# Three attention heads of four turned on VectorE and by SBUF to SBUF transfers, in a fused Perceiver, Mamba and MoE layer

## The chip, the cores and the metric

The kernel runs on one core of a Trainium2 chip. The metric is the device time of one execution in microseconds; the median of the runs shown is quoted. A core has TensorE (PE in the profile, its weight loads PEld), VectorE (DVE), ScalarE (ACT), GpSimd (POOL) and SyncE (SP), each of which works through its own instructions in order, and 16 DMA engines. Nearly all transfers of this kernel are issued by SyncE, one after the other.

## What is computed

All numbers are float32. Only the first of three stages is touched by the change, cross-attention of 16 sequences of 128 queries over 2048 context rows, 16 heads of 32:

```python
x = x + xattn(layernorm(x), ctx)          # x (16,128,512), ctx (16,2048,512)
x = x + mamba_block(layernorm(x))         # in_proj, conv, scan over 16 states, out_proj, MLP
x = x + moe(layernorm(x))                 # 8 experts' gates, one shared and one expert weight

# xattn
q = queries @ wq.T + bq
k = context @ wk.T + bk
v = context @ wv.T + bv
attn = softmax(q k^T * HD ** -0.5)        # per head
out = (attn v) @ wo.T + bo
```

## The kernel before

The order of the work is written out by hand: a loop over time steps u (line 1329) issues on every engine what belongs to that step, and each engine takes its instructions in the order in which they were issued. Steps 0 to 255 are the attention: step u is sequence u // 16, block u // 4 % 4 of 512 context rows, and head group u % 4, four heads. Beside it runs the rest: keys and values of the next block (group "made"), from step 54 on the scan of the Mamba stage for pairs of sequences ("decays", "inputs", "scan"), and "late" work put at fixed steps (queries, output projection, in-projection, out-projection). After step 256 come the remaining scans and the feed-forward.

**One attention step.** `scores` (L302): four matmuls, one for each head, into four PSUM banks of 512 columns. `weighted` (L378): the weighted sums of step u-1 for the heads turned on TensorE, and of step u-2 for the heads turned by transfer. `maxima` (L312): VectorE takes the row maximum of each bank (L315). `exps` (L319): ScalarE takes the exponential of each bank into `pr` (L325). The exponentials must be turned, with context rows on partitions, before they can be weights of the sums. Two ways are used for it, with ND = 2 and NP = 4 - ND = 2:
- `turn` (L353): heads 0 to NP-1, four 128x128 transposes a head on TensorE (L357) and a copy by ScalarE into `pT` (L359).
- `blocks` (L334): the last ND heads, one VectorE instruction that transposes 32x32 blocks into `tr` (L337, one buffer), which goes to a DRAM tile `trd` (L341, one transfer). `gathered` (L343), in the next step: four transfers bring it back, blocks in their places, as `pd` (L347).

**Keys and values.** A block's 512x512 context product is done in seven products of quarter size (a Strassen-like scheme) instead of eight, for keys in steps with u % 4 = 1 and 2, for values in those with 3 and 0. `load_ctx` (L151) loads the four quarters c00, c10, c11, c01 of the block's context, 256 KB each; c01 has one buffer, the others two. `ctx_sums` (L225) forms four differences on GpSimd in steps u % 4 = 1 (L236): t1 = c01 - c00, t2 = c11 - t1, t3 = c11 - c01, t4 = c10 - t2; in steps with u % 16 = 5 all four stand together, otherwise `dt_third` and `inputs` of the scan (L686 to L698) stand between t2 and t3. `product` (L238) puts products into two PSUM banks, pa and pc (L244). In a step, `x_products` come after the sums (phase 0: c00 and c10; phase 1: t3 into pa, t1 into pc), `y_products` at the end of the step (phase 0: t2 into pa; phase 1: t4 into pa, c11 into pc). `hold` (L282) copies pa to SBUF on ScalarE (L285), and `k_sum` (L253) and `v_sum` (L268) add pc and a held copy on VectorE (L264, L274), with the key bias bk in L264. `y_sums` (L295) writes the last quarter from pa on ScalarE (L262, L272).

**SyncE's order in a step** is that of the calls: `gathered(u-1)`, `step_loads` (L1338: x, dt weights, the scan's row broadcast `bc` at offset 0, L647, 512 KB), then, after the transpose of the step, `trd`, and `later_loads` (L1343: `bc` at offset 16, weights, context). Context quarters are asked for in these steps:

```python
if u % 4 == 1 and made + 1 < B * SB:
    load_ctx(made + 1, ("c00", "c10", "c11"))
if u % 4 == 2 and made + 1 < B * SB:
    load_ctx(made + 1, ("c01",))
```

with made = (u + 3) // 4, so each quarter is asked for three or four steps before it is used.

**The scan's time step.** `dt_first` (L662) takes |v|, exp(-|v|) on ScalarE and max(v, 0) on VectorE (L672); `dt_second` (L677) takes the logarithm into a tile of its own, `l`. `values_kept` (L362) copies the value columns that the transferred heads of head group 3 need one step longer.

Of the kernel before, what the change touches and what calls it, by code (L numbers as in the profile page):

```python
# [15 lines left out]
P = 128  # L16
# [15 lines left out]
ND = 2  # L32
# [4 lines left out]
def perceiver_layer(ctx: ExitStack, tc: tile.TileContext, a: dict, out: bass.AP):  # L37
# [23 lines left out]

    trd = [dram.tile([P, ND * 512], FP, tag=f"trd{i}", name=f"trd{i}") for i in range(2)]

# [49 lines left out]
    with ExitStack() as es:  # L113
# [15 lines left out]
        banks = [psum.tile([P, 512], FP, tag=f"s{j}", name=f"bank{j}") for j in range(4)]  # L129
# [21 lines left out]
        def load_ctx(g, names=("c00", "c10", "c11", "c01")):  # L151

            for n in names:
                j, c = int(n[1]), int(n[2])
                t = pool.tile(
                    [P, 2, 256], FP, tag=n, name=f"{n}_{g}", bufs=1 if n == "c01" else 2
# [68 lines left out]
        def ctx_sums(g, names):  # L225
            b11, b12, b21, b22 = (ctx_t[g, j, c] for j in range(2) for c in range(2))
            for n in names:
                t = pool.tile([P, 2, 256], FP, tag=n, name=f"{n}_{g}", bufs=1)
# [24 lines left out]
        def k_sum(g, o, c, pc, x):  # L253
            for r in range(2):
                hg = 2 * o + r
                if (g, hg) not in kts:
                    kts[g, hg] = pool.tile(
                        [P, 512], FP, tag=f"kt{hg}", name=f"kt{g}_{hg}", bufs=1 + (hg == 3)
                    )
                t = kts[g, hg][:, c * 256 : (c + 1) * 256]  # L260
                if pc is None:
# [20 lines left out]
        def hold(key, g, pa, tag):  # L282
            n = ND if tag == "tr" else 1
            t = pool.tile([P, 2 * n, 256], FP, tag=tag, name=f"{tag}{key}{g}", bufs=1)[:, 0:2, :]
            nc.scalar.copy(t, pa)  # L285
            held[key] = t
# [8 lines left out]
        def y_sums(of, g, ph, pa, pc, tag="u2"):  # L295
            if ph == 0:
                hold(of + "u2", g, pa, tag)
# [4 lines left out]
        def scores(u):  # L302
# [7 lines left out]
            del kts[u // 4, hg]  # L310

        def maxima(u):  # L312
            b, sb, hg = split(u)
            for j in range(4):
                nc.vector.tensor_reduce(  # L315
                    stats[b][0][j][:, sb, hg : hg + 1], banks[j], AX.X, ALU.max, negate=True
                )

        def exps(u):  # L319
# [3 lines left out]
            for j in range(4):  # L323
# [5 lines left out]
                    bias=nm[j][:, sb, hg : hg + 1],  # L329
# [4 lines left out]
        def blocks(u):  # L334
# [6 lines left out]
            nc.sync.dma_start(trd[u % 2], t.rearrange("p c h i q -> p (c h i q)"))  # L341

        def gathered(u):  # L343

            pd = pool.tile([P, 4, ND, 4, 32], FP, tag="pd", name=f"pd{u}", bufs=1)
            for c in range(4):
                nc.sync.dma_start(  # L347
                    pd[c * 32 : (c + 1) * 32].rearrange("k a h i q -> k a (h i q)"),
                    trd[u % 2].rearrange("(a k) (c r) -> c k a r", k=32, c=4)[c],
                )  # L350
            pds[u] = pd
# [41 lines left out]
        def weighted_out(u):  # L393
            b, sb, hg = split(u)
            if hg == 3:
                t = keep.tile([P, 4, P], FP, tag="avs", name=f"avs{b}_{sb}", bufs=4)
                nc.scalar.copy(t[:, 0:3, :], avp[:, 0:3, :])
                nc.scalar.copy(t[0 : NP * HD, 3, :], avp[0 : NP * HD, 3, :])
                avs[b, sb] = t

        def weighted_last(u):
            b, sb, hg = split(u)
            if hg == 3:
                nc.scalar.copy(avs[b, sb][NP * HD :, 3, :], avp[NP * HD :, 3, :])
# [9 lines left out]
        def normal(b):  # L414
# [10 lines left out]
            nm = [keep.tile([P, SB, 4], FP, tag=f"nm{j}", name=f"nm{b}_{j}") for j in range(4)]  # L425
# [34 lines left out]
        def joined(b):  # L460
# [3 lines left out]
            for j in range(4):  # L464
                nc.vector.tensor_copy(
# [1073 lines left out]
```

## Time and profile before

| what | value |
|---|---|
| median of 3 runs | 3578.6 us (3576.97 to 3579.74) |
| the profiled execution's own time | 3579.3 us |
| its span in the trace | 3577.5 us |
| granted TensorE clock, mean | 0.995 of full speed |
| busy: TensorE, VectorE, GpSimd, ScalarE | 98%, 75%, 69%, 64% |
| DMA: bytes moved, mean rate | 816.79 MB, 228 GB/s |
| one cycle of 32 steps with scans | 367.0 us |
| in a cycle: DMA busy share, rate | 79%, 249 GB/s |

The busy share of an engine is an average over the stages. A group of instructions is named by its line, engine and operation, and by the tiles that it writes and reads. The chain of waits follows the work that ended last back in time, at each step to what released it. A timeline row gives start, length, engine, line, operation, tiles, count, and in brackets the idle time before it with what ended that. SPq rows are transfers as SyncE issues them; the time from issue to landing is given apart.

### The profile page before, as it was taken

What the parts mean: (1) busy time and instruction counts of PE and PEld (TensorE: products, weight loads), DVE (VectorE), ACT (ScalarE), POOL (GpSimd) and SP (SyncE); (2) the same over time, 40 slices, a digit from 0 to 9 for tenths busy, and PEclk for the clock granted to TensorE, in tenths of its full rate; (3) what the DMA queues carried; (4) which work ended last, traced back from release to release, by engine and by line L of the source; (5) the groups of instructions that cost most, each with busy time, mean ns of one, the idle gap of its engine ahead of it and who ended that gap; (6) DMA issues with size and microseconds to landing.
All of it is one profiled execution on the core that took longest, in us unless ns stands there. A gap on an engine that the chain in (4) does not pass through costs nothing.

```text
span 3577.5 us, 68547 instructions
## 1 busy us (share of the span) xinstructions
PE 3518.9 (98%) x24072; PEld 2638.5 (74%) x24072; DVE 2672.0 (75%) x4390; ACT 2285.5 (64%) x5672; POOL 2462.7 (69%) x2353
## 2 busy tenths in 40 slices
PE   8999999999999999999999999999999989999999
PEld 6777787778777877787778777877777756656655
DVE  4555556897889788978797879887988767668743
ACT  3555556777677766777677767776777665545422
POOL 2111214896889788978797779777987778789920
PEclk9999999999999999999999999999999999999999
DMA  4444445787788778787788778778777887676742
GB/s 146 159 148 154 159 152 193 250 265 220 254 251 268 233 253 256 252 243 247 250 257 247 231 257 265 240 224 271 254 245 224 266 300 254 219 273 245 260 173 77
DMA packets 527541, 816.79 MB, mean 228 GB/s; under 512 B 44848, under 2 KB 378960, under 8 KB 526944
## 3 DMA queue, kind: packets, MB, share of 16 engines
q1 hardware_dynamic: 526752, 811.79, 70.4%
q8 instruction: 192, 3.15, 0.3%
q14 instruction: 149, 1.22, 0.1%
q0 software_dynamic: 448, 0.63, 0.1%
HBM read 661.51 MB, written 150.73 MB: 227 GB/s over the span
## 4 chain that ended last, share of the span: by engine, by line
PE 86%; DVE 4%; POOL 4%; DMA 3%; ACT 3%; issue 1%; SPq 0%; DVEq 0%; POOLq 0%
PE pa L244 24%; PE pc L244 17%; PE bank L307 7%; PE avp L385 7%; PE bank L577 6%; PE bank L357 6%; PE bank L986 3%; PE bank L762 3%; PE bank L955 2%; PE bank L1087 2%; PE bank L515 2%; ACT pr L325 1%; POOL w L698 1%; DMA bc<-bcd 1%; PE bank L442 1%
## 5 line engine op out<-in xcount | busy, mean ns | idle before, releaser
L325 ACT ACTIVATE pr<-bank,nm 128x512 f32<-128x512 f32 x1024 | 688.5, 684 | 199.3 <-DVE nm L315 197.3
L315 DVE TENSOR_REDUCE nm<-bank 128x1 f32<-128x512 f32 x1024 | 633.8, 678 | 60.0 <-PE bank L307 59.6
L698 POOL TENSOR_TENSOR w<-dx,bc 128x512 f32<-128x512 f32 x512 | 648.1, 1287 | 30.7 <-DMA bc<-bcd 22.6
L749 POOL TENSOR_TENSOR ysum<-ysum,w 128x512 f32<-128x512 f32 x384 | 500.4, 1303 | 229.4 <-DVE hst L712 205.9
L719 ACT ACTIVATE hst<-dt,alog 128x254 f32<-128x254 f32 x918 | 442.4, 482 | 71.5 <-DVE hst L712 39.1
L337 DVE STREAM_TRANSPOSE tr<-pr 128x1024 f32<-128x1024 f32 x256 | 318.8, 1245 | 119.9 <-ACT pr L325 110.3
L735 POOL TENSOR_TENSOR w<-w,bc 128x512 f32<-128x512 f32 x256 | 329.1, 1286 | 76.6 <-DVE w L734 74.0
L385 PEld LDWEIGHTS avp<-pT,v 128*32 128x32 f32 x4096 | 204.4, 110 | 198.3 <-issue 194.2
L734 DVE TENSOR_TENSOR_SCAN w<-hst,w 128x512 f32<-128x512 f32 x256 | 309.5, 1209 | 40.0 <-ACT hst L719 33.2
L236 POOL TENSOR_TENSOR t<-c,c 128x512 f32<-128x512 f32 x128 | 164.3, 1283 | 232.3 <-PE pc L244 135.6
L359 ACT COPY pT<-bank 128x512 f32<-128x512 f32 x512 | 271.7, 581 | 48.9 <-PE bank L357 48.8
L307 PE MATMUL bank<-kt,qT 32*128 32x512 f32 x2048 | 301.3, 641 | 1.6 <-ACT pT L359 1.6
L385 PE MATMUL avp<-pT,v 128*32 128x128 f32 x4096 | 276.4, 277 | 1.5 <-ACT pT L359 1.4
L357 PE MATMUL bank<-ident,pr 128*128 128x128 f32 x2048 | 266.2, 273 | 0.8 <-ACT pr L325 0.7
L357 PEld LDWEIGHTS bank<-ident,pr 128*128 128x128 f32 x2048 | 239.1, 141 | 27.7 <-ACT pr L325 2.5
L734 DVE TENSOR_TENSOR_SCAN hst<-hst,w 128x512 f32<-128x512 f32 x203 | 247.8, 1221 | 7.1 <-ACT hst L719 7.1
L244 PE MATMUL pa<-t,ks 128*128 128x256 f32 x1024 | 248.6, 386 | 0.0
L244 PE MATMUL pa<-vs,t 128*128 128x256 f32 x1008 | 244.8, 386 | 0.0
L577 PE MATMUL bank<-zT,win 128*128 128x256 f32 x992 | 224.8, 379 | 0.0
L244 PEld LDWEIGHTS pa<-t,ks 128*128 128x128 f32 x1024 | 185.9, 190 | 36.0 <-issue 13.8
L244 PEld LDWEIGHTS pa<-vs,t 128*128 128x128 f32 x1008 | 183.0, 190 | 35.6 <-ACT hst L719 9.9
L385 PE MATMUL avp<-pd,v 128*32 128x128 f32 x3072 | 205.8, 276 | 3.2 <-DMA pd<-trd 3.2
(315 smaller groups left out, 7709.8 us busy)
## 6 DMA issues: line engine op xcount, KB each, us to landing
bc<-bcd SPq DMA_DIRECT2D x512, 512.0 KB, 5.3
trd<-tr SPq DMA_DIRECT2D x256, 512.0 KB, 3.8
pd<-trd SPq DMA_DIRECT2D x1024, 128.0 KB, 2.9
c<-in_ctxT_dram SPq DMA_DIRECT2D x256, 256.0 KB, 6.0
wf<-in_w_dram SPq DMA_DIRECT2D x124, 512.0 KB, 6.7
wqo<-in_wqkvo_dram SPq DMA_DIRECT2D x128, 256.0 KB, 6.3
win<-in_win_dram SPq DMA_DIRECT2D x128, 256.0 KB, 5.9
wout<-in_wout_dram SPq DMA_DIRECT2D x128, 256.0 KB, 6.2
```

The lines of the kernel that those rows point to most:

```text
L244: nc.tensor.matmul(ps[:, r, :], l[:, kc, r * P : (r + 1) * P], m[:, kc, :], start=(i in (1, 2, 5) and r == 0 and kc == 0), stop=(r == 1 an ...
L307: nc.tensor.matmul(banks[j], qts[b][rows, hg, :], kts[u // 4, hg][rows, :], start=True, stop=True)
L315: nc.vector.tensor_reduce(stats[b][0][j][:, sb, hg : hg + 1], banks[j], AX.X, ALU.max, negate=True)
L325: nc.scalar.activation(pr[:, j, :], banks[j], AF.Exp, bias=nm[j][:, sb, hg : hg + 1], accum_out=sm[:, sb, h : h + 1],)
L357: nc.tensor.transpose(ps[:, i, :], prs[u][:, j, i * P : (i + 1) * P], ident)
L385: nc.tensor.matmul(avp[j * HD : (j + 1) * HD, v % 4, :], values(v, i, j), pts[v, j][:, i, :] if j < NP else pds[v][:, :, j - NP, i, :], st ...
L577: nc.tensor.matmul(ps, w[:, kc, :], zTs[g][:, kc, :], start=(kc == 0), stop=(kc == KC - 1))
L698: nc.gpsimd.tensor_tensor(w, dx.unsqueeze(1).to_broadcast([P, NH // 2, GT]), bcs[g * 32 + r, 0][:, i * NH // 2 : (i + 1) * NH // 2, :], AL ...
L719: nc.scalar.activation(bt(h[:, k, :])[:, :, 1:], bt(dt)[:, :, 1:], AF.Exp, scale=aneg[:, ec, n : n + 1],)
L734: nc.vector.tensor_tensor_scan(y if i else x, y, x, 0.0, ALU.mult, ALU.add)
L735: eng.tensor_tensor(w, to, bcs[g * 32 + r, DS][:, i * NH // 2 : (i + 1) * NH // 2, :], ALU.mult)
L749: nc.gpsimd.tensor_tensor(s, s, w, ALU.add)
```

## The change

- ND becomes 3 and NP 1: three heads are turned by VectorE's block transpose and by transfers, one on TensorE. The buffers of `tr`, `pd`, `pT` and `vh` follow from ND and NP; `pd` gets two buffers for one, `tr` keeps one.
- The DRAM tile `trd` and `gathered` go. `blocks` issues sixteen transfers at once, from `tr` to `pd` in SBUF, 32 partitions x 1536 bytes each (48 KB). They stand in SyncE's order after the transpose of their step, ahead of the weights and context of that step.
- Both `bc` broadcasts are now in `step_loads`, ahead of the transpose of their step.
- t3 is written over c01. c00, c10 and c01 have one buffer, c11 two. The quarters are asked for in steps u % 4 = 0 (c01), 1 (c11) and 3 (c00, c10).
- Banks 2 and 3 are one PSUM tile; one reduction takes both maxima.
- kt0 and kt1 are one tile, and the bias of these two key groups is added on ScalarE as the held copy is made (two instructions for one copy); VectorE adds pc to both in one instruction.
- max(v, 0) of the time step becomes a Relu on ScalarE, and the logarithm is written in place.
- The copy of the weighted sums is split otherwise, and the banks for late work are given out in another order.

```diff
-ND = 2
+ND = 3
-        banks = [psum.tile([P, 512], FP, tag=f"s{j}", name=f"bank{j}") for j in range(4)]
+        banks = [psum.tile([P, 512], FP, tag=f"s{j}", name=f"bank{j}") for j in range(2)]
+        pairs = att.enter_context(tc.tile_pool(name="pairs", bufs=1, space=PSUM))
+        pair = pairs.tile([P, 2, 512], FP, tag="s23", name="pair")
+        banks += [pair[:, 0, :], pair[:, 1, :]]
...
-                    [P, 2, 256], FP, tag=n, name=f"{n}_{g}", bufs=1 if n == "c01" else 2
+                    [P, 2, 256], FP, tag=n, name=f"{n}_{g}", bufs=2 if n == "c11" else 1
...
-                t = pool.tile([P, 2, 256], FP, tag=n, name=f"{n}_{g}", bufs=1)
+                if n == "t3":
+                    t = b12
+                else:
+                    t = pool.tile([P, 2, 256], FP, tag=n, name=f"{n}_{g}", bufs=1)
...
+                if o == 0:
+                    if r == 0:
+                        nc.vector.tensor_tensor(
+                            kts[g, "01"][:, :, c * 256 : (c + 1) * 256], pc, x, ALU.add
+                        )
...
-            nc.scalar.copy(t, pa)
+            if biased:
+                for r in range(2):
+                    nc.scalar.activation(
+                        t[:, r, :], pa[:, r, :], AF.Identity, bias=bk[:, r : r + 1]
+                    )
+            else:
+                nc.scalar.copy(t, pa)
...
-            for j in range(4):
+            for j in range(2):
...
+            nc.vector.tensor_reduce(
+                stats[b][0][2][:, sb, hg, :], pair, AX.X, ALU.max, negate=True
+            )
...
-            nc.sync.dma_start(trd[u % 2], t.rearrange("p c h i q -> p (c h i q)"))
-
-        def gathered(u):
-
-            pd = pool.tile([P, 4, ND, 4, 32], FP, tag="pd", name=f"pd{u}", bufs=1)
-            for c in range(4):
-                nc.sync.dma_start(
-                    pd[c * 32 : (c + 1) * 32].rearrange("k a h i q -> k a (h i q)"),
-                    trd[u % 2].rearrange("(a k) (c r) -> c k a r", k=32, c=4)[c],
-                )
+            pd = pool.tile([P, 4, ND, 4, 32], FP, tag="pd", name=f"pd{u}", bufs=2)
+            for a_ in range(4):
+                for c in range(4):
+                    nc.sync.dma_start(
+                        pd[c * 32 : (c + 1) * 32, a_].rearrange("k h i q -> k (h i q)"),
+                        t[a_ * 32 : (a_ + 1) * 32, c].rearrange("k h i q -> k (h i q)"),
+                    )
...
-            nc.vector.tensor_scalar(dt, ps, dtb[:, ec : ec + 1], 0.0, ALU.add, ALU.max)
+            nc.scalar.activation(dt, ps, AF.Relu, bias=dtb[:, ec : ec + 1])
...
                 load_bc(u + 2 - 32 - LAG, 0)
+                load_bc(u + 1 - 32 - LAG, DS)
 
             def later_loads():
-                load_bc(u + 1 - 32 - LAG, DS)
                 for f in weights.get(u, ()):
                     f()
-                if u % 4 == 1 and made + 1 < B * SB:
-                    load_ctx(made + 1, ("c00", "c10", "c11"))
-                if u % 4 == 2 and made + 1 < B * SB:
-                    load_ctx(made + 1, ("c01",))
+                names = (("c01",), ("c11",), (), ("c00", "c10"))[u % 4]
+                if u and made + 1 < B * SB:
+                    load_ctx(made + 1, names)
...
-                gathered(u - 1)
...
-            free = banks[NP:]
-            places = [(free + banks)[i] for i in range(len(after_turns))]
-            if live and len(after_turns) > len(free):
-                if u % 4 == 0:
-                    places = [flat(avp), *places[:-1]]
-                elif u % 2 and makes and u not in behind:
-                    places[-1] = flat(pc)
+            free = [banks[1], banks[2], banks[0], banks[3]]
+            places = free[: len(after_turns)]
```

## What was predicted before the run

> **What bounds the kernel now.** First the page. Its chain of work that ended last is nearly all TensorE, and the busy row agrees:
>
> ```profile
> PE 3518.9 (98%) x24072; PEld 2638.5 (74%) x24072; DVE 2672.0 (75%) x4390; ACT 2285.5 (64%) x5672; POOL 2462.7 (69%) x2353
> ...
> PE 86%; DVE 4%; POOL 4%; DMA 3%; ACT 3%; issue 1%; SPq 0%; DVEq 0%; POOLq 0%
> ```
>
> Second, the 256 attention steps. Counted from one score matmul (L307) to the next, a step u lasts 8.34 us if u is odd and 10.06 if it is even, plus its "late" work; eight groups of four steps make a cycle of 367.0 us, in which TensorE is busy 364.4, VectorE 305.8, GpSimd 300.4, ScalarE 265.4. The chain from 1796 to 1836 us is TensorE without a gap:
>
> ```profile
> 1806.79 1.07 PE bank L307 x8
> 1807.86 1.02 PE avp L385 x32
> 1808.88 1.92 PE pa L244 x8
> 1810.80 1.73 PE pc L244 x8
> 1812.53 0.87 PE bank L357 x8
> 1813.40 1.73 PE pa L244 x8
> 1815.13 1.07 PE bank L307 x8
> ```
>
> This is step 161: scores, weighted sums, two x products, eight transposes (two heads), one y product. So time taken from TensorE is gained only while nothing else arrives late. Third, therefore, what could: the turn's path through VectorE and SyncE's queue, in the timeline.
>
> ```profile
> 1802.21 1.25 DVE L337 STREAM_TRANSPOSE tr<-pr 128x1024 f32<-128x1024 f32 x1 [0.43 <-ACT pr L325]
> 1807.46 1.27 POOL L236 TENSOR_TENSOR t<-c,c 128x512 f32<-128x512 f32 x1
> 1808.81 1.26 POOL L236 TENSOR_TENSOR t<-c,t 128x512 f32<-128x512 f32 x1
> ...
> 1817.27 1.90 SPq L347 DMA_DIRECT2D pd<-trd  x4
> ...
> 1822.21 0.34 SPq L341 DMA_DIRECT2D trd<-tr  x1
> 1823.04 0.32 SPq L647 DMA_DIRECT2D bc<-bcd  x1
> 1823.41 0.71 SPq L158 DMA_DIRECT2D c<-in_ctxT_dram  x1
> ```
>
> The last line is quarter c01 of the next group's context, asked for in step 162 and used in step 165 by t1 = c01 - c00 on GpSimd (the L236 rows; for group 41 at 1807.46). That is three steps of notice. Below, T is the end of the VectorE transpose in a step and S the start of its scores.
>
> **Relief.** Four of eight transposes go: 0.87/2 = 0.43 us a step, 13.9 a cycle, 111 over 256 steps. ScalarE loses one of two copies L359 (0.53). That is the whole gain on the binding engine.
>
> **Cost 1, the longer transpose.** 1536 for 1024 columns: 1.25 x 1.5 = 1.87, so +0.62 on VectorE. Given back there: the pair's maximum in one reduction (L315 has a pitch of 0.62; at most 0.1 saved), kt0 and kt1 in one add (0.83 to 0.67, twice in four steps), the time step's maximum (L672, 0.47 each fourth step). VectorE comes to about 9.9 us a step: no bound by itself. But an even step's last product needs pc, which VectorE's sum frees after the transpose: scores start at S, transpose starts at S + 5.55 and ends T = S + 7.42, sum 0.67 to 0.83, 0.1 of hand-over, product 1.73 and 0.1 to the next scores; next S = T + 2.6 to 2.8 = S + 10.05. TensorE alone would need 10.06 - 0.43 = 9.63. In steps 2 and 3 of a group the exponentials start 1.9 after S and the third now waits for the pair's maximum, about 0.37. Over a cycle the even steps without much late work give 3.7 back.
>
> **Cost 2, context quarter c01 comes late.** In the new order t3 is written over c01, which has one buffer, so c01 can be loaded only after the last product with t3, in step 4n; it is used in step 4n+1. On SyncE it stands behind the sixteen transfers of step 4n (and, where there are any, that step's weights), and the first of these waits for the transpose. So it is issued a burst after T.
> - Burst: 16 issues. A lone issue took 0.32 + 0.045 of gap (L639, L660: 32 rows), four of L347 in a row 0.43 + 0.045 (128 pieces). In rows back to back 128, 256 and 512 pieces cost 0.475, 0.57 and 0.77 (L347, L158, L547); 32 pieces lie near the lone row. Ends 0.365 and 0.475, I take 0.38: 6.1 us (5.8 to 7.6).
> - Landing of c01: the answers for L158 give
>
> ```profile
> DMA to landing us min/median/max: 3.2/3.9/6.0
> DMA to landing us min/median/max: 4.5/6.2/9.4
> ```
>
>  from 60 to 540 us and from 700 to 2800. There the single load follows a 512 KB broadcast (L647); now it follows 48 KB pieces. Ends 3.2 and 6.2; I take 3.5, nearest to the quiet rows (3.3 for the single loads there).
> - So c01 is there at T + 9.6. t1 and t2 take 2.6 (the two L236 rows), and the y product with t2 and the hand-over 1.95: the next scores start at T + 14.2, where T + 2.6 + 8.34 - 0.43 = 10.5 was due. 3.7 lost. GpSimd works in order: dt_third (2.4) and inputs (L698, 2.51) stand between t2 and t3 (1.3), so with the gaps between them t3 is there at T + 18.7, while the next step's first product wants it at 14.2 + 2.1 = T + 16.3: 2.4 more. In groups with u % 16 = 5 t3 follows t2 at once, but four wqo loads (0.51 each) stand ahead of c01. Late work in the step (3.46 for an in-projection L577, 6.88 for an out-projection L762, in the chain) hides as much.
> - Lost in the eight groups of a cycle, by u % 32: 1: 3.7 + 2.4; 5: 4.3; 9: 1.7 + 2.4; 13: 0 (step 12 is 17.1 long); 17: 2.0 + 2.4; 21: 5.2; 25: 0.3 + 2.4; 29: 0.5 + 2.4; less what Cost 1 has counted in the same steps (about 2): 28 a cycle. In the 54 steps before the scans (no dt_third, no inputs) 39.
>
> **Cost 3, one tr buffer.** The next transpose overwrites tr and must wait until all sixteen transfers have landed. Cycle: 1.87 + 15 x 0.38 + landing + 0.1. For a 48 KB SBUF to SBUF transfer there is no row; L774 (256 KB out) has 2.0 at least and 2.5 in the median, L347 2.8, L341 2.9. Ends 2.0 and 2.9, I take 2.3: 10.0 us a step (9.5 to 12.0). Two plain steps were due in 18.1, so the transposes of a plain pair come up to 1.9 late, and through Cost 1 so do its scores: 4.5 a cycle, 17 in the first 54 steps, where plain steps are the rule.
>
> A transfer that goes out also waits for the one eight places before it, in the program; at 8 x 0.38 = 3.0 a landing of 2.3 to 2.9 hides that, one behind two broadcasts would not: up to 1 us a burst, kept for the range. A landing under 2.0 us is not excluded (L639 shows 1.5 once), but is not a gain by itself: below 9.2 us a step the buffer no longer binds.
>
> The Trainium skill speaks against this change: "DMA: Bandwidth & Descriptors", Rules for kernel authors, says to coalesce small transfers, since under 64 KB one pays mostly overhead. Before, the rows are one issue of 512 KB and four of 128 KB; the new ones are of 48 KB. The page's fixed part of about 2.0 us (Anatomy of one DMA, stated for another issuing path) would make Cost 3 9.7 us a step, an estimate, and the sum some 15 us smaller.
>
> **What costs nothing.** The key bias moves into the held copies: two of four holds are 0.82 for 0.59 (L262, L285), ScalarE has gained 0.53 a step; the next pa product comes 0.7 after the hold, which covers 0.23. Relu on ScalarE: 0.42 each fourth step, same cover. bc at 16 moves ahead of the burst, past SyncE's weights; it is wanted a step later. If the burst stood before it, it would be short of time like c01. c00 and c10, asked for in step 4n+3, land near T + 11 and are wanted at about T + 13; c11 has two buffers. With c01 late, a broadcast's buffer comes free about 1 us late on GpSimd and delays a burst: range. The kept values are 96 columns wide for 64: 0.3 on GpSimd each fourth step, which is 82% busy. Nothing after 2850 us changes.
>
> **Sum.** A cycle: -13.9 + 3.7 + 28 + 4.5 = +22. Steps 54 to 255 are 6.3 cycles: +141. The first 54 steps: -23 + 7 + 39 + 17 = +40. Together +181 on a span of 3577.5, with the 1.8 outside it (own time 3579.3, median 3578.6): 3577.5 + 1.8 + 181 = 3760.
>
> **Range.** All lower ends (0.365, 3.2, 2.0): c01 is 0.55 earlier in the 54 groups that nothing covers (30) and Cost 3 15 smaller: 3715. All upper ends (0.475, 6.2, 2.9): c01 4.2 later in those groups (227), Cost 3 at 12 us a step (2 us more in some 60 plain pairs, 125): 4110.
>
> **Rivals.**
> 1. *Forecast*: c01 late and the buffer cycle. 0.72. Speaking for it: program order, and both times are well over what is due.
> 2. *All transfers hidden, faster*: c01 lands by T + 6.0, so that t2 and its product are done when step 4n+1 ends anyway, and bursts end within a plain step. Place: GpSimd's t1. It decides at a burst plus landing of 6.0 us, where the shortest rows give 5.8 + 3.2 = 9.0. Then only the relief and Cost 1 remain: -111 + 30 = -81, 3498. Against it, each row. 0.10.
> 3. *Only the buffer cycle counts*, because c01 lands in time by a way I misread: -81 + 70 = -11, 3568 (Cost 3 counts 70, not 45, where c01 does not stretch the same steps; 3540 to 3860 with its ends). 0.08.
> 4. *SyncE as the bound*: issues at 0.475 and landing behind queues, 4110; from 0.44 on its burst and loads fill the plain step. Against it: DMA was busy 79% in these stages, and 256 KB a step fewer are moved. 0.10.
>
> The range takes the forecast, reaches halfway from its lower end to rival 3 (3640) and most of the way to its upper end and rival 4 (4000); left out are rival 2, most of rival 3 and a little of 4, 0.20. About 0.2% (7 us) is what a measurement of this kernel can tell from no change. Faster 0.13 (rival 2 and a part of 3), same 0.05, slower 0.82.
>
> **What would show it.** Right: GpSimd's t1 waits on a DMA of c01 some 6 us in most groups; TensorE's pa product (L248 in the new numbering) waits on GpSimd; StreamTranspose waits on the pd transfers; steps 4n+1 of 12 us and more; TensorE busy falls by 111 us and its share below 94%. Wrong: sixteen issues in under 4 us, c01 landed before GpSimd arrives, or TensorE still without gaps; then the time is below 3579.

## The result and the profile after

The changed kernel takes 4785.3 us (median of 4 runs, 4781.21 to 4789.97) against 3577.9 us for the kernel before on the same chip: a ratio of 1.337, interval 1.335 to 1.340. It is 1207 us slower. The forecast said slower, 3760 us, at most 4000. The direction and the places of the waits were right; the price was too low by a factor of more than six.

| | before | after |
|---|---|---|
| median, us | 3577.9 | 4785.3 |
| span of the profiled execution | 3577.5 | 4779.4 |
| first 54 attention steps | 550.4 | 779.1 |
| from there to the start of step 255 | 2294.6 | 3249.5 |
| from the start of step 255 on | 689.4 | 709.2 |
| a cycle of 32 steps | 367.0 | 520.4 |
| granted TensorE clock, mean | 0.995 | 0.898 |

The page of the changed kernel: the busy row, and the two rows on the chain that ended last (share of the span by engine, then by line).

```profile
PE 3778.8 (79%) x23048; PEld 2707.1 (57%) x23048; DVE 2721.7 (57%) x3926; ACT 2229.4 (47%) x5544; POOL 2464.1 (52%) x2353
...
SPq 27%; PE 26%; DMA 23%; POOL 8%; issue 7%; DVE 6%; ACT 3%; DVEq 0%; POOLq 0%
SPq L367 24%; DMA bc<-bcd 15%; PE pa L248 6%; DMA pd<-tr 4%; PE pc L248 3%; PE bank L1006 3%; DVE tr L360 3%; POOL w L718 2%; POOL t L240 2%; PE bank L326 2%; PE bank L975 2%; PE bank L1107 2%; PE avp L405 1%; DMA c<-in_ctxT_dram 1%; DMA wout<-in_wout_dram 1%
```

SyncE's queue (SPq), which had 0% of the chain, now has the largest share, nearly all in one line: the sixteen transfers (L367). TensorE falls from 98% to 79% of its time. The groups on the same page show who waits (busy and mean ns, then idle time before them and what ended it), and the last line gives the median landing of the new transfers, in us.

```profile
L360 DVE STREAM_TRANSPOSE tr<-pr 128x1536 f32<-128x1536 f32 x256 | 455.2, 1778 | 884.0 <-DMA pd<-tr 706.2
...
L240 POOL TENSOR_TENSOR t<-c,c 128x512 f32<-128x512 f32 x64 | 80.9, 1265 | 1269.9 <-DMA c<-in_ctxT_dram 780.5
...
pd<-tr SPq DMA_DIRECT2D x4096, 48.0 KB, 1.9
```

Both waits that the forecast named are there: the transpose waits for the transfers that still read `tr`, and GpSimd's t1 for a context quarter. How long SyncE takes to issue a transfer is in the trace's answer for line 367 (duration in ns: shortest, median, longest):

```profile
L367 SPq DMA_DIRECT2D pd<-tr x4096: 507/589/2302, 48.5 to 4099.5; - x196
```

0.589 us, and 0.044 us of gap to the next: 0.63 us an issue, where the forecast took 0.38. SyncE's own timeline (start, duration, line) shows what that makes of a step:

```profile
2000.34 10.70 SPq L367 DMA_DIRECT2D pd<-tr  x16
2011.14 1.04 SPq L159 DMA_DIRECT2D c<-in_ctxT_dram  x2
2012.27 0.89 SPq L668 DMA_DIRECT2D bc<-bcd  x2
2014.51 12.31 SPq L367 DMA_DIRECT2D pd<-tr  x16
2026.92 0.53 SPq L159 DMA_DIRECT2D c<-in_ctxT_dram  x1
2027.55 0.89 SPq L668 DMA_DIRECT2D bc<-bcd  x2
2030.15 10.70 SPq L367 DMA_DIRECT2D pd<-tr  x16
```

Sixteen issues take 10.1 us, or more where a broadcast is in the way: SyncE's waits (us in total, times, longest) have

```profile
SPq L367 <- DMA bc<-bcd: 262.8, 232, 2.9
```

and the 256 bursts last 11.7 us on average, 11.0 in the median. With broadcasts and loads SyncE has 12 to 14 us of work for a step that was due in 8 to 10. VectorE's timeline of the same stretch gives the other half of the loop; in brackets is the idle time ahead of the transpose.

```profile
2012.67 1.78 DVE L360 STREAM_TRANSPOSE tr<-pr 128x1536 f32<-128x1536 f32 x1 [5.03 <-DMA pd<-tr]
...
2028.31 1.78 DVE L360 STREAM_TRANSPOSE tr<-pr 128x1536 f32<-128x1536 f32 x1 [4.96 <-DMA pd<-tr]
```

From the end of one transpose to the end of the next, steps 3 to 254 never take less than 13.3 us, half of them 14.8 or less. The forecast's own formula gives just that floor with the measured durations: 1.78 + 15 x 0.633 + 1.9 + 0.1 = 13.3. Last, the end of that step on GpSimd and on TensorE: quarter c01, issued at 2026.92 behind its burst and landed at 2029.65, then t1 (its row names no releaser, but it starts 0.12 us after that landing), and the product that needs t2.

```profile
2029.77 1.27 POOL L240 TENSOR_TENSOR t<-c,c 128x512 f32<-128x512 f32 x1 [11.29 <-issue]
```

```profile
2032.44 3.78 PE L248 MATMUL pa<-t,ks 128*128 128x256 f32 x8 [7.57 <-POOL t L240]
```

The eight matmuls take 3.78 us after that idle time; the last product of the next step, at 2042.52 and with no wait ahead of it, takes 1.89.

### The profile page after: what moved, and what is told of

It is laid out like the page before. It is cut to its first block, busy times and chain, and to the rows that moved or that the text cites. A ratio compares the mean times of both kernels' runs of the same rounds, so it can differ in the third digit from the quotient of the medians.

```text
span 4779.4 us, 69601 instructions
## 1 busy us (share of the span) xinstructions
PE 3778.8 (79%) x23048; PEld 2707.1 (57%) x23048; DVE 2721.7 (57%) x3926; ACT 2229.4 (47%) x5544; POOL 2464.1 (52%) x2353
## 4 chain that ended last, share of the span: by engine, by line
SPq 27%; PE 26%; DMA 23%; POOL 8%; issue 7%; DVE 6%; ACT 3%; DVEq 0%; POOLq 0%
SPq L367 24%; DMA bc<-bcd 15%; PE pa L248 6%; DMA pd<-tr 4%; PE pc L248 3%; PE bank L1006 3%; DVE tr L360 3%; POOL w L718 2%; POOL t L240 2%; PE bank L326 2%; PE bank L975 2%; PE bank L1107 2%; PE avp L405 1%; DMA c<-in_ctxT_dram 1%; DMA wout<-in_wout_dram 1%
## 5 line engine op out<-in xcount | busy, mean ns | idle before, releaser
L360 DVE STREAM_TRANSPOSE tr<-pr 128x1536 f32<-128x1536 f32 x256 | 455.2, 1778 | 884.0 <-DMA pd<-tr 706.2
L240 POOL TENSOR_TENSOR t<-c,c 128x512 f32<-128x512 f32 x64 | 80.9, 1265 | 1269.9 <-DMA c<-in_ctxT_dram 780.5
L335 DVE TENSOR_REDUCE nm<-bank 128x1 f32<-128x512 f32 x512 | 328.8, 683 | 338.3 <-PE pair L326 334.6
L348 ACT ACTIVATE pr<-bank,nm 128x512 f32<-128x512 f32 x512 | 347.8, 686 | 215.9 <-DVE nm L335 214.8
L348 ACT ACTIVATE pr<-pair,nm 128x512 f32<-128x512 f32 x512 | 348.0, 688 | 42.6 <-DVE nm L338 42.5
L755 POOL TENSOR_TENSOR w<-w,bc 128x512 f32<-128x512 f32 x256 | 326.2, 1274 | 57.4 <-DVE w L754 57.4
L326 PE MATMUL pair<-kt,qT 32*128 32x512 f32 x1024 | 333.6, 732 | 0.0
L300 ACT ACTIVATE u2ku<-pa,bk 128x256 f32<-128x256 f32 x128 | 53.8, 471 | 578.3 <-PE pa L248 578.2
L338 DVE TENSOR_REDUCE nm<-pair 128x2 f32<-128x1024 f32 x256 | 310.6, 1213 | 0.0
L248 PE MATMUL pc<-vs,c 128*128 128x256 f32 x504 | 162.7, 480 | 140.5 <-DVE v L287 140.5
L598 PE MATMUL bank<-zT,win 128*128 128x256 f32 x544 | 163.2, 454 | 123.7 <-DMA win<-in_win_dram 123.1
L405 PE MATMUL avp<-pd,v 128*32 128x128 f32 x4608 | 224.6, 292 | 12.1 <-DMA pd<-tr 10.2
```

The lines of the kernel that those rows point to most:

```text
L248: nc.tensor.matmul(ps[:, r, :], l[:, kc, r * P : (r + 1) * P], m[:, kc, :], start=(i in (1, 2, 5) and r == 0 and kc == 0), stop=(r == 1 an ...
L326: nc.tensor.matmul(banks[j], qts[b][rows, hg, :], kts[u // 4, hg][rows, :], start=True, stop=True)
L335: nc.vector.tensor_reduce(stats[b][0][j][:, sb, hg : hg + 1], banks[j], AX.X, ALU.max, negate=True)
L348: nc.scalar.activation(pr[:, j, :], banks[j], AF.Exp, bias=nm[2][:, sb, hg, j - 2 : j - 1] if j > 1 else nm[j][:, sb, hg : hg + 1], accum_ ...
L360: nc.vector.transpose(t.rearrange("p c h i q -> p (h i) c q"), prs[u][:, NP:, :].rearrange("p h (i c k) -> p (h i) c k", i=4, c=4),)
L405: nc.tensor.matmul(avp[j * HD : (j + 1) * HD, v % 4, :], values(v, i, j), pts[v, j][:, i, :] if j < NP else pds[v][:, :, j - NP, i, :], st ...
```

## The experiments

The theory after the result: SyncE's issues, at 0.63 us, are the cause, by way of the one `tr` buffer (the 13.3 us floor) and of what stands behind them in the queue. Rivals: the late quarter c01 by itself; the moved `bc` broadcast; the small edits. Where a run leaves out part of the work, its expectation says which. A time without an interval is that of one run; the kernel before took 3576 to 3585 us on the same chips.

### 1. Only the late quarter undone: e1_c01_early

```diff
-                names = (("c01",), ("c11",), (), ("c00", "c10"))[u % 4]
+                names = ((), ("c11",), (), ("c00", "c10"))[u % 4]
...
+            if u and u % 4 == 0 and makes and made + 1 < B * SB:
+                load_ctx(made + 1, ("c01",))
             if live:
                 blocks(u)
```

> The changed kernel, but SyncE asks for context quarter c01 ahead of the sixteen transfers of its step instead of behind them; nothing else is moved. Theory Q (a transfer from SBUF to SBUF holds SyncE for 0.63 us, so that a burst takes 10.1 us and the single tr buffer lets a step be no shorter than 1.8 + 9.5 + 1.9 + about 0.4 = 13.6 us): the wait of GpSimd's t1 on c01 goes, from 780 us to under 100, but steps stay at 13.6 or more, in sum about 4300 us (4220 to 4400). Rival C (c01's lateness is what costs, the burst is hidden behind it): steps fall to under 11 us, in sum 3570 to 3700.

Measured: 4751.8 us, 34 less. The wait of t1 on context falls from 780 to 296 us, and VectorE's wait on the transfers rises from 706 to 1001:

```profile
DVE tr L360 <- DMA pd<-tr: 1001.1, 190, 11.0
...
POOL t L240 <- DMA c<-in_ctxT_dram: 296.1, 14, 56.0
```

So the quarter is no cause by itself at sixteen transfers: what it cost was waited for anyway. The fall to 4220 to 4400 did not come. That range took the steps to lie near the floor; they last 15.7 us on average from transpose to transpose, as against 15.8 in the changed kernel, and only 44 of 255 are under 13.6.

### 2. What makes an issue dear: e5_rows1024, e7_four_transfers, e8_dram_source

Three kernels change one side of the transfer each: the row (two heads, 1024 B; edit `ND = 2`), the count and the rows of one transfer, and the source.

```diff
 # e7_four_transfers
-                for c in range(4):
-                    nc.sync.dma_start(
-                        pd[c * 32 : (c + 1) * 32, a_].rearrange("k h i q -> k (h i q)"),
-                        t[a_ * 32 : (a_ + 1) * 32, c].rearrange("k h i q -> k (h i q)"),
-                    )
+                nc.sync.dma_start(
+                    pd[:, a_].rearrange("k h i q -> k (h i q)"),
+                    t[:, a_].rearrange("k h i q -> k (h i q)"),
+                )
 # e8_dram_source
-                        t[a_ * 32 : (a_ + 1) * 32, c].rearrange("k h i q -> k (h i q)"),
+                        a["ctxT"][b, a_][c * 32 : (c + 1) * 32, 0, 0 : ND * P],
```

> The changed kernel with two heads instead of three by VectorE and sixteen SBUF to SBUF transfers: rows of 1024 bytes instead of 1536, 32 partitions as before, c01 behind the burst as in the change. If the time of an issue is fixed by there being SBUF on both sides, it stays at 0.59 + 0.04 us and the time stays near 4700 (4600 to 4800). If it goes with the bytes of a row (or with a row length that is no power of two), it falls to 0.43 to 0.5 + 0.04, a burst to 8 us, and the time to 4200 to 4400.

> The changed kernel with the sixteen transfers joined to four of 128 rows of 1536 B (pd[:, a] from tr[:, a]); the same bytes, and it leaves out the exchange of the 32-row blocks between partition groups, so the sums use exponentials of other keys. Theory 'a fixed cost for each issue' (0.59 us busy + 0.04 of gap, sixteen times): a burst is 2.5 to 3 us, transpose to transpose takes at least 1.8 + 3 + 2.5 + 0.4 = 7.7 us, so neither tr nor the late quarter binds much: 3550 to 3800 us. Rival 'a cost for each row' (0.63 us for 32 rows): each issue takes 2.3 us, the burst stays near 10 us, 4650 to 4800 us. Rival 'the bc broadcast and the quarter in front of the burst, not the issues': 4300 to 4700 us, with a burst under 4 us and long waits for the landing.

> The changed kernel with the sixteen transfers reading 32 rows of 1536 B from the context in DRAM instead of tr; it leaves out moving the exponentials, the sums use context rows as weights. tr is no longer read by a transfer, so its buffer does not wait. Theory 'SBUF on both sides makes the issue dear': an issue takes 0.32 to 0.43 us as in the rows of the kernel before, burst 6 to 7.6 us, 3700 to 4200 us. Rival 'the shape of 32 rows makes it dear, whatever the source': 0.55 to 0.6 us an issue, burst about 10 us, 4400 to 4750 us.

Measured: 4689.3, 3667.7 and 4151.0 us. The issue durations, from the answers for the transfers' line of e5, e7 and e8, in this order:

```profile
L367 SPq DMA_DIRECT2D pd<-tr x4096: 507/588/2038, 48.3 to 4009.2; - x196
```

```profile
L366 SPq DMA_DIRECT2D pd<-tr x1024: 464/598/1856, 48.8 to 2987.7; - x171
```

```profile
L368 SPq DMA_DIRECT2D pd<-in_ctxT_dram x4096: 310/419/2911, 30.2 to 3472.8; - x196
```

A shorter row changes nothing (0.588), four times the rows change nothing (0.598), and DRAM as the source takes it to 0.42. So an issue from SBUF to SBUF costs about 0.59 us whatever its size here, and one with DRAM on one side less. With four issues 1118 of the 1207 us are gone. All three times lie in the ranges of the theory. e5 shows one thing more: with only two heads moved this way the kernel takes 4689 us, so nearly the whole loss comes with the sixteen transfers and not with the third head.

### 3. The time against the length of the burst: e12_eight_transfers, e14_four_c01_early, e19_eight_c01_early

e12 has eight transfers of 64 rows; e14 and e19 are e7 and e12 with the edit of e1.

```diff
 # e12_eight_transfers
-                for c in range(4):
+                for c in (0, 64):
                     nc.sync.dma_start(
-                        pd[c * 32 : (c + 1) * 32, a_].rearrange("k h i q -> k (h i q)"),
-                        t[a_ * 32 : (a_ + 1) * 32, c].rearrange("k h i q -> k (h i q)"),
+                        pd[c : c + 64, a_].rearrange("k h i q -> k (h i q)"),
+                        t[c : c + 64, a_].rearrange("k h i q -> k (h i q)"),
```

> The changed kernel with eight transfers of 64 rows of 1536 B in place of sixteen of 32 rows; it leaves out the exchange of blocks between partition groups, the sums use exponentials of other keys. The issue was 0.60 us for 128 rows and 0.59 for 32, so a burst is 8 x 0.63 = 5.0 us; transpose to transpose at least 1.8 + 4.4 + 2.1 + 0.4 = 8.7 us, under most steps. Theory 'the count of issues sets the time, and binds where burst and landing pass a plain step': 3700 to 3900 us, near the 3668 of four transfers and far from 4785. Rival 'time in proportion to the count': halfway on the line from 4 to 16 transfers, 3668 + 4/12 x 1117 = 4040 us.

> The kernel of e7_four_transfers (four transfers of 128 rows, without the exchange between partition groups) with quarter c01 asked for ahead of the transfers in step 4n, behind the last product with t3. Theory 'the late quarter is what is left there' (GpSimd waited 361 us for context quarters in e7): c01 comes 2.5 us earlier and the wait falls by half or more, 3520 to 3610 us. Rival 'c01 is late because it may be written only after that product, wherever it stands in the queue': 3640 to 3680 us.

> The kernel of e12_eight_transfers (3930 us; eight transfers of 64 rows, without the exchange between partition groups) with quarter c01 asked for ahead of them. Theory 'a burst that fits into a step costs by the late quarter alone': c01 comes 5 us earlier, 3560 to 3640 us. Rival 'SyncE's issues hold other loads too': 3720 to 3900 us.

Measured, with the burst as count x (median issue + 0.044 us):

| transfers | burst, us | c01 behind the burst | c01 ahead of it |
|---|---|---|---|
| 4 (e7, e14) | 2.6 | 3667.7 | 3551.1 |
| 8 (e12, e19) | 5.1 | 3929.9 | 3716.3 |
| 16 from DRAM (e8) | 7.4 | 4151.0 | not run |
| 16 (after, e1) | 10.1 | 4785.3 | 4751.8 |

The burst of the table leaves out waits. With them the median burst lasts 2.4 us in e7, 5.5 in e12, 10.3 in e8 and 11.0 in the changed kernel: the bursts from DRAM wait for broadcasts too. The late quarter is worth 117 us at four transfers, 214 at eight, and 34 at sixteen, where it hides. e14 is the only one below the kernel before, by 28 us, and it does not compute the layer, since the blocks stay in their partitions. Its TensorE has 97% of its time and the clock is 0.994, so the freed transposes do come back as time once the rest is out of the way. e12 came out 30 us above the range of its theory, nearer to it than to the 4040 of its rival. In e19 the theory that a burst that fits into a step costs by the quarter alone was wrong: 165 us stay with eight transfers though c01 is early (3716 against 3551), and GpSimd still waits 244 us for context and 159 for transfers. My reading is that SyncE's queue delays other loads too; the wait for context alone does not show it, for e14 has 215 us of it.

### 4. The buffer or SyncE itself: e16_tr_two, e17_other_source

```diff
 # e16_tr_two
...
-            t = pool.tile([P, 4, ND, 4, 32], FP, tag="tr", name=f"tr{u}", bufs=1)
+            t = pool.tile([P, 4, ND, 4, 32], FP, tag="tr", name=f"tr{u}", bufs=2)
-            pd = pool.tile([P, 4, ND, 4, 32], FP, tag="pd", name=f"pd{u}", bufs=2)
+            pd = pool.tile([P, 4, ND, 4, 32], FP, tag="pd", name=f"pd{u}", bufs=1)
 # e17_other_source
-                        t[a_ * 32 : (a_ + 1) * 32, c].rearrange("k h i q -> k (h i q)"),
+                        xproj[a_ * 32 : (a_ + 1) * 32, 0 : ND * P],
```

> The changed kernel with two tr buffers and one pd buffer (the same room), sixteen transfers as before. The transpose no longer waits for the sixteen to land. Theory 'SyncE's own time is the bound': each step still holds 16 x 0.63 + about 1 to 2 us of broadcasts and loads, 11 to 12 us, so steps fall from 13.5 and more only to about 12, 4450 to 4700 us. Rival 'the one tr buffer is the bound': steps fall to what is due, 3900 to 4300 us. Rival 'pd with one buffer takes its place': no change, 4750 to 4850 us, with the transfers waiting for the weighted sums.

> The changed kernel with the sixteen transfers reading 32 rows of 1536 B of another SBUF tile (the projection weights) in place of tr; it leaves out moving the exponentials, the sums use those weights. Count, size and sides of the transfers stay, so a burst should stay near 10 us; but no transfer reads tr, so the transpose waits for none of them, and they do not wait for it. Theory 'the one tr buffer is the part above 7.4 us': the slope of about 95 us per us of burst goes on, 4151 + 2.7 x 95 = 4400 us (4300 to 4500). Rival 'SyncE's own time binds every step': 4650 to 4800 us. Rival 'the tr buffer is all of it': under 4000 us.

e16 took 5728.3 us and tells nothing about `tr`: `pd` is read two steps after the transpose, so with one buffer the transfers wait for the weighted sums, as SyncE's waits say (us in total, times, longest):

```profile
SPq L367 <- PE avp L405: 1551.7, 251, 15.2
```

My third rival there had the right place, but I had taken it for free. e17 took 4586.5 us: 199 us less without the buffer's wait, between the ranges of the theory (4300 to 4500) and of SyncE as the bound (4650 to 4800). Its timeline shows SyncE at work without a pause:

```profile
1999.75 0.37 SPq L668 DMA_DIRECT2D bc<-bcd  x1
2000.21 14.17 SPq L367 DMA_DIRECT2D pd<-xproj  x16
2014.43 1.28 SPq L568 DMA_DIRECT2D win<-in_win_dram  x2
2015.75 0.62 SPq L159 DMA_DIRECT2D c<-in_ctxT_dram  x1
2016.41 0.46 SPq L681 DMA_DIRECT2D dtw<-in_dtproj_dram  x1
2016.97 0.84 SPq L668 DMA_DIRECT2D bc<-bcd  x2
2017.91 14.24 SPq L367 DMA_DIRECT2D pd<-xproj  x16
```

The two whole bursts here take 14.2 us (12.1 is the median in e17), since a transfer also waits for one that was issued earlier and has not landed; mostly that is a broadcast, as SyncE's waits in e17 say:

```profile
SPq L367 <- DMA bc<-bcd: 367.9, 344, 2.7
```

So with the buffer free SyncE takes over at nearly the same pace. In the changed kernel the buffer is a part of 199 us, not the whole. e17 and e8 together are the cleanest test of the issue: neither waits for `tr`, both have sixteen transfers of the same size, and with the source in SBUF (0.588 us an issue) the kernel takes 436 us more than with the source in DRAM (0.419).

### 5. The moved broadcast: e9_bc_back, e18_early_and_back

```diff
                 load_bc(u + 2 - 32 - LAG, 0)
-                load_bc(u + 1 - 32 - LAG, DS)

             def later_loads():
+                load_bc(u + 1 - 32 - LAG, DS)
```

> The changed kernel with one edit undone: the second half of the bc broadcasts is asked for behind the sixteen transfers again, not ahead of them. Theory 'sixteen issues of 0.63 us are the bound': the same number of issues, transpose to transpose stays at 13.5 us and more; the broadcast now comes later, 4750 to 4950 us. Rival 'the moved broadcast holds the burst back' (bursts of 12.3 us behind two broadcasts against 10.7 us, and DMA bc in 15% of the chain): bursts all near 10.7 us, 4400 to 4650 us.

> The changed kernel with both reorderings, c01 ahead of the sixteen transfers and the second half of the bc broadcasts behind them. Alone they gave 4752 and 4707 for 4785. Theory 'the burst of 10 us and the one tr buffer hold every step at 13.5 us and more': 4600 to 4720 us. Rival 'the two together clear the way': under 4400 us.

Measured: 4707.3 and 4649.9 us. Undoing the move gives 78 us, between the two ranges that I had written. The bursts did fall to 10.7 us in the median, as the rival said, but that brought little, for GpSimd now waits 367 us for the broadcasts (`w`, L755). With c01 early as well it is 135 us, as the theory had it. The floor of 13.3 us stays in both. The move costs, but little beside the burst.

### 6. The small edits alone: e11_small_only, e11b_small_clean, e15_small_no_pair

All three turn two heads through DRAM as before. e11 has all small edits, the broadcast's move and the changed kernel's places for late work; e11b keeps the order of before; e15 is e11b without the joined bank tile, so that four banks and four maxima stand as before:

```diff
 # e15_small_no_pair against e11b_small_clean
-        banks = [psum.tile([P, 512], FP, tag=f"s{j}", name=f"bank{j}") for j in range(2)]
-        pairs = att.enter_context(tc.tile_pool(name="pairs", bufs=1, space=PSUM))
-        pair = pairs.tile([P, 2, 512], FP, tag="s23", name="pair")
-        banks += [pair[:, 0, :], pair[:, 1, :]]
+        banks = [psum.tile([P, 512], FP, tag=f"s{j}", name=f"bank{j}") for j in range(4)]
...
```

> The small edits alone: two heads by VectorE and DRAM as before, context loaded early as before (all quarters two buffers), but with t3 written over c01, one tile for banks 2 and 3 with one maximum, kt0 and kt1 in one add with the bias in the held copies, Relu on ScalarE. Theory Q: nothing but a few us, 3565 to 3590. Rival E: 3650 and more.

> The kernel before with the small edits alone: last two score banks one tile with one maximum, kt0 and kt1 one tile, key bias in the held copies, time step's maximum on ScalarE; two heads by VectorE through DRAM, bc broadcasts and late work in the order of before. Prediction's 'what costs nothing': 3560 to 3590 us. Rival 'the joined tiles and the biased holds add waits in each step' (the third exponential waits for the pair's maximum, 0.37 us in two steps of four): 3620 to 3700 us. Rival 'e11_small_only was slow by them': over 3850 us.

> The kernel before with the small edits but without the joined bank tile: kt0 and kt1 one tile, key bias in the held copies, time step's maximum on ScalarE, the logarithm in place; two heads through DRAM. e11b_small_clean lost all its time in steps with late work, where two in-projections in the two halves of one tile waited for each other, and none in the first plain steps. Theory 'that alone was its loss': 3560 to 3590 us here. Rival 'the biased holds or the one kt01 buffer cost in the late steps': 3620 to 3900 us.

Measured: 3934.0 us (ratio 1.098, 1.096 to 1.100), 3915.6 us (1.095, 1.090 to 1.099) and 3584.7 us (1.0016, 1.0007 to 1.0026). The key bias in the holds, the joined kt0 and kt1 and the time step on ScalarE thus cost 5 us. The first two were misses: the loss is the joined tile's, together with the places of before. In e11b the plain steps from 2 on take 8.3 and 10.1 us as in the kernel before; steps with late work grow from 11.8 to 16.0, and there two in-projections stand in the two halves of one tile:

```profile
ACT zs L633 <- PE pair L604: 249.2, 56, 5.3
```

That the halves wait for each other because they are one tile is my reading; what is shown is that the loss goes with the tile (e15). e11 has the changed kernel's places, whose first bank its second turned head uses; how its loss divides between that and the broadcast's move was not tried. The changed kernel takes banks 1, 2, 0, 3 in this order, with one head on TensorE, and a step with two pieces has them in different tiles. There the wait of `zs` for the tile is 70 us in 48 times, 2.3 at most, near the 64 of the kernel before, and e14 has the same tile and places and is faster than the kernel before; so this loss is hardly part of the 1207 us.

### 7. Three heads by another way: e4_dram3, e6_dram3_bc_back, h4_mixed, h8_mixed

e4 and e6 keep DRAM (one write, four reads) for three heads, with all quarters early; e6 has the broadcast back behind the write. h4 and h8 send one or two of the four block columns directly and the rest through DRAM, with c01 early and the broadcast back.

```diff
 # h4_mixed
+            nc.sync.dma_start(
+                trd[u % 2], t[:, 1:].rearrange("p c h i q -> p (c h i q)")
+            )
             for a_ in range(4):
-                for c in range(4):
+                for c in range(1):
...
+        def gathered(u):
+
+            for c in range(1, 4):
+                nc.sync.dma_start(
+                    pds[u][c * 32 : (c + 1) * 32].rearrange("k a h i q -> k a (h i q)"),
+                    trd[u % 2].rearrange("(a k) (c r) -> c k a r", k=32, c=3)[c - 1],
+                )
```

> Three heads turned by VectorE as in the changed kernel, with all its small edits, but moved as before by one write to DRAM and four reads of 128 KB rows each step, and all context quarters with two buffers, asked for three to four steps early as before. Theory Q: SyncE is held 2.2 us a step, as before; no wait of the transpose on transfers, and the sum is the relief of 111 us less the longer transpose's 30: about 3500 us (3480 to 3540), a little more if the 256 KB that a step moves in addition make transfers late. Rival E (the small edits cost: the pair of banks as one tile, the bias in two instructions, Relu on ScalarE): it stays well over 3578.

> Three heads by VectorE, but by one write to DRAM and four reads, context quarters early with two buffers, and (other than in e4_dram3) the second half of the bc broadcasts back behind the write and the reads. Theory 'the moved broadcast delays the write of tr': the write lands in about 4 us as before instead of 8.0, steps 54 to 255 take 2250 to 2330 us, 3480 to 3560 us in all, faster than the kernel before (Relief 111 less Cost 1 of 30). Rival 'the 1.5-fold DRAM traffic fills the DMA engines': the write still lands at 7 us or later, 3720 to 3810 us. Rival 'TensorE clock': TensorE busy time does not fall by 111 us because its granted clock is lower; 3580 to 3700 us.

> Three heads by VectorE, a quarter of the blocks by four SBUF to SBUF transfers and three quarters through DRAM (one write of 576 KB, three reads of 192 KB), c01 ahead of them and the bc broadcasts as in the kernel before. SyncE issues 0.4 + 4 x 0.63 = 2.9 us behind the transpose and 1.3 for the reads; the DRAM traffic is 1.1 times that of the kernel before, against 1.5 times in e6_dram3_bc_back (3644). Theory 'few issues and less traffic': 3520 to 3600 us. Rival 'c01 with one buffer stays late' (88 us in e7_four_transfers): 3620 to 3720 us. Rival 'the reads come too late behind the burst': over 3720 us.

> As h4_mixed (3643 us), with half of the blocks by eight SBUF to SBUF transfers and half through DRAM (one write and two reads). SyncE issues 0.4 + 8 x 0.63 = 5.4 us behind the transpose and 0.9 for the reads. Rival A 'the DMA traffic holds the mixed way': less of it, 3560 to 3630 us. Rival B 'SyncE's issues hold it': 3680 to 3850 us.

| kernel | us | ratio to before | 95% interval |
|---|---|---|---|
| e4_dram3 | 3804.8 | 1.063 | 1.061 to 1.065 |
| e6_dram3_bc_back | 3644.0 | 1.018 | 1.017 to 1.020 |
| h4_mixed | 3643.2 | 1.017 | 1.013 to 1.021 |
| h8_mixed | 3922.3 | 1.095 | 1.092 to 1.097 |

None beats the kernel before, and none came out as its theory said: e4, e6 and h4 were to take 3480 to 3600 us. The write of `tr` landed in 3.8 us in the median before, 8.0 in e4 and 5.2 in e6, as the answers for its line say:

```profile
DMA to landing us min/median/max: 3.2/8.0/10.7
```

```profile
DMA to landing us min/median/max: 3.2/5.2/9.0
```

So the moved broadcast, ahead of the write, costs 161 us on this way. What e6 still loses may be the traffic's. The DMA row of its page (busy share in tenths, 40 slices):

```profile
DMA  5777768999989899999999999999999987676752
```

Through most of the scans the 16 engines are busy 90% and more; before it was 79% in a cycle. But the write lands in 5.2 us, not in 7 or later as the rival of the traffic had it, and 3644 lies in the range of the rival of the clock: TensorE is busy 29 us less than before, where 112 us of its work are gone, at a mean clock of 0.987. h4 moves less through DRAM and takes the same time. So what holds e6 and h4 is not shown. h8 moves still less through DRAM and is slower than h4, so traffic does not explain it; what points to SyncE's issues is that its `tr` waits 175 us for the transfers again, GpSimd 297. Rival B had the place and too small a price. e4 and e6 serve the forecast in one more point: their first 54 steps, without scans and broadcasts, take 529.5 and 530.0 us for 550.4, 20 to 21 less.

## Why the prediction was right and wrong

**Relief: right.** The four transposes a step that are left take 153.7 us where eight took 266.2: 112.5 gone for the 111 predicted. In e14 that becomes time: 530.8 us for the first 54 steps.

**Cost 1: right.** The longer transpose takes 1.78 us for the estimated 1.87. The first 54 steps of e4, e6 and e14 are 20 us shorter; the forecast's own -23 + 7 says 16.

**Cost 2 and Cost 3: the failed step is the issue interval.** The text says "Ends 0.365 and 0.475, I take 0.38: 6.1 us (5.8 to 7.6)". It is 0.63 us, and the burst 10.1, 4.0 more than the 6.1 taken; both lie outside their ends. Two readings failed. The smaller: 32 rows in a burst were put near a lone issue, 0.32 us, but one of the two rows named for that, L660, has 0.427 in the median and 0.326 only as its least:

```profile
L660 SPq DMA_DIRECT2D dtw<-in_dtproj_dram x64: 326/427/2050, 556.1 to 3346.7; - x64
```

Its 44 issues close behind another transfer have a median of 0.43, the 20 others 0.33. In e8, with bursts of 32 rows from DRAM, it is 0.42, which makes 7.4 us, near the upper end of the forecast: 1.3 of the 4.0. The other 2.7 come from the memory. All rows used for the ends were transfers with DRAM on one side, and were chosen by their number of rows. The runs show that between two SBUF tiles the count of rows does not matter (32 or 128: 0.59 and 0.60) and the sides do (0.42 from DRAM). No row of before had SBUF on both sides, and a bound from unlike rows was no bound. The landing, 1.9 us, was slightly better than the 2.3 taken. With the right interval the formula of Cost 3 gives 13.3 us a step, which the trace has as its floor, where 10.0 was written. Taking 13.3 us as the least for each step of before that is shorter (and 0.43 off the others) makes the 255 distances 3445 us for 2845: +600 of the 1184 us by which these steps grew. No run prices the rest. Part of it is the waits behind broadcasts inside the bursts: with the mean burst of 11.7 us the formula gives 14.9 us a step, an estimate, and the mean from transpose to transpose is 15.8.

**Cost 2, c01: right in kind, smaller in effect.** t1's wait and the wait of `pa` on GpSimd are there. It was priced at 215 us (28 a cycle and 39). But two late things overlap: the early quarter gives 34 us at sixteen transfers and 117 and 214 at four and eight.

**"What costs nothing": right but for the broadcast.** Bias, Relu and kt01 cost 5 us (e15). The move of `bc` costs 78 us (e9), and 161 where the write of `tr` stands behind it (e6 against e4). The "up to 1 us a burst" behind broadcasts, kept for the range, is there: 263 us in 232 waits, 1.1 us each.

**Rivals.** Rival 4, SyncE as the bound from 0.44 us on, is what happened; it had 0.10 and the price of an end that was itself too low. At 0.46 us (e8) the kernel takes 4151 us, near the 4110 written for 0.475, but that is luck: 125 us and more of that sum are the wait for `tr`, which e8 does not have, and its bursts last 10.3 us. Rivals 2 and 3 fell: nothing was hidden.

**The rule against this change** was weighed and then used only for the landing. The Trainium skill's "DMA: Bandwidth & Descriptors", Rules for kernel authors, to coalesce small transfers, agrees with e7: the same bytes in four transfers take 3668 us for 4785. The same page, under Issuing engines are not separate DMA queues, calls the sequencer's time to initiate a DMA "usually small relative to the DMA itself"; here it is 0.63 us of the 1.9 from issue to landing, a third, and sixteen of them, 10.1 us, follow one after the other, and the measurement decides.

**What stays open.** The TensorE clock. TensorE is busy 260 us longer than before although it does 112.5 us less: its matmuls are slower after idle times (562 ns on average in the group of pa<-t,ks, 384 in the same group of e14). In these five kernels the mean clock falls with the busy share of TensorE: 0.994 at 97% in e14, 0.962 at 90% in e12, 0.941 at 87% in e8, 0.898 at 79% after, 0.835 at 69% in e16. How much of it lies on the path and how much fills time that was idle anyway, no run separates. Nor was a second `tr` buffer beside two of `pd` tried, nor an issue of the transfers by another engine than SyncE. The 1207 us are thus attributed to the issues (1118 go with four of them), of which 199 go through the `tr` buffer and 78 meet the moved broadcast, but these parts overlap and do not add up.

## What to carry to other kernels

Price a transfer by a row that has the same memory on both sides; if there is none, keep the range open to twice the nearest row, and ask what the kernel takes at that end. Multiply issue time by the count before anything else: a queue that issues for everyone is an engine like the others, and when its work passes the shortest step, the loads behind it come late too. Take the time of an issue from issues in a row, not from a lone one. Where a buffer's reader is a burst, its cycle is transpose + burst + landing; with the buffer's wait gone (e17) that was worth 199 of the 1207 us here, for the queue had no time left.

## What the hardware showed

- An SBUF to SBUF transfer took 0.59 to 0.60 us in the median to issue on SyncE, whether of 32, 64 or 128 rows and of 1024 or 1536 B a row; from DRAM to SBUF, with the same 32 rows, 0.42 in the median and 0.31 at least.
- Such a transfer of 48 KB landed in 1.9 us in the median, of 192 KB in 2.3 (e7).
- Bursts waited for broadcasts of 512 KB issued ahead of them: 263 us in the changed kernel, 368 in e17.
- The mean granted TensorE clock was 0.994 where TensorE was busy 97% of the time (e14), and 0.835 where it was busy 69% (e16).
